# Adding up queries and keys by quarters in a two-level Winograd projection

## The chip, the cores and the metric

The kernel runs on one core of a Trainium2 chip. A core has five engines that run beside each other, each with a queue of its own that it works off strictly in order: TensorE (PE in the profile; PEld is its loading of weights), VectorE (DVE), ScalarE (ACT), GpSimd (POOL) and SyncE (SP), which here only issues DMAs. Engines wait for one another by semaphores. The metric is the device time of one execution in microseconds, as the median of several runs.

## The reference

The reference is a transformer layer over 32 sequences of 64 tokens, 512 wide: self-attention with 32 heads of 128, cross-attention over a context of 128, and a mixture of expert biases. Only the self-attention's front part matters here:

```
q = rmsnorm((hidden @ Wq + bq).reshape(b, n, H, HD), gq)
k = rmsnorm((hidden @ Wk + bk).reshape(b, n, H, HD), gk)
v = (hidden @ Wv + bv).reshape(b, n, H, HD)
attn = softmax(einsum("bnhd,bmhd->bhnm", q, k) * HD ** -0.5)
out = einsum("bhnm,bmhd->bnhd", attn, v) @ Wo + bo
```

`rmsnorm` divides by the root of the mean of the squares over the 128 numbers of a head. All of it is float32.

## The kernel before, in words

The 2048 tokens are split into two halves of 1024, a half into two units of 512 tokens (`t` = 0 and 1). The 32 heads are taken in 16 groups of two (`hg`). For each half and each group the kernel makes queries, keys and values of both units. Group 0 of each half goes through a simpler path (`single`); the other 15 of each half, 30 in all, go through `double`, and one such pass is called a window here.

**The products.** In a window the queries and keys come from a matrix product in two levels of Winograd's form of Strassen's scheme: seven products instead of eight outside, and again seven inside each. `Window.project` runs the outer products in four rounds, n = 0 to 3: products 1 and 5, then 2 and 6, then 7 and 3, then 4 alone. `Window.outer` runs the inner ones of each round in four steps, m = 0 to 3. A place (n, m) in this text is step m of round n. In each step TensorE multiplies into one or two of three PSUM banks (`p_w` in the profile, line 655), and VectorE takes a bank over into the unit's tile `qk` in SBUF: `keep` (line 666) adds the bank to what another part of the tile already holds, `end` (line 679) adds a bank to the place itself. Inside a round the bank `pa` is not cleared between products: TensorE adds the next product to what is in it. So it may not go on with `pa` before `keep` has read it. In round 3 this is so between place (3, 0), whose `keep` reads `pa`, and place (3, 1), whose first product is added to it.

A unit's `qk` tile has four places of 128 x 512: place 2h + ab holds head h, half ab of the unit's tokens; the first 256 of the 512 numbers are queries (j = 0), the last 256 keys (j = 1). A quarter of the result of a round is one t and one j.

**The outer sums.** Winograd's scheme ends with sums over whole results: place 2 takes place 3 in, and then place 3 takes place 1 in. `add` does this after round 2: for unit 0 on GpSimd, for unit 1 on VectorE (both line 734, 128 x 512). Then `squares` (ScalarE, line 356) squares each place, and at the window's end TensorE adds the squares up over a head (`ms_w`, line 779), from which the roots for `rmsnorm` come. Round 3 changes place 1 only, in place: the `keep` of (3, 0) for t = 0, j = 0 writes what GpSimd's second sum reads.

**What sets the order.** The orders on PE, VectorE, ScalarE and GpSimd are written out by hand: each engine gets its instructions in the order in which the Python code calls them. After each step of `outer`, `project` first calls what the dictionary `behind` holds for the place, then one piece of waiting work (`take_waiting`: scaling of queries for an earlier unit on VectorE, line 544, or a part of a softmax), and then what `plan` holds for it: `v`, one of the seven steps of the values' product (`values`, lines 387, 403 and 407), `line.scale` (keys of an earlier unit times their roots on GpSimd, line 542), `line.turn`, or `make`, which has GpSimd work out sums of the next group's weights (lines 120 and 152 to 155). In a window's round 2, `line.scale` is called at (2, 0), and `make` at (2, 3), where four sums of 128 x 384 are left over (lines 152 to 155). In group 1, sums of the input (lines 345 and 346 on GpSimd) are called at (2, 1) too. In group 15 there are no weight sums at (2, 3).

The values use a PSUM bank `va` in the same way: ScalarE's copy (`keep` in `values`, line 403) must have read it before TensorE goes on in it. The values' third step, at (2, 2), has such a copy, and the fifth, at (3, 0), goes on in the bank; the fifth has one again, and the sixth, at (3, 1), goes on in it.

Of the kernel before, what the change touches and what calls it, by code (L numbers as in the profile page):

```python
# [10 lines left out]
ALU = mybir.AluOpType  # L11
# [30 lines left out]
def decoder_layer(  # L42
# [228 lines left out]
    def take_waiting():  # L271
        if waiting:
            waiting.pop(0)()
# [80 lines left out]
    def square(of, name, part=1):  # L354
        sq = squares_tile(f"sq{name}", part)
        nc.scalar.activation(sq, of, AF.Square)  # L356
        return sq
# [266 lines left out]
    class Window:  # L624
# [86 lines left out]
        def project(self, plan):  # L711

            units, hg = self.units, self.w.hg
            for unit in units:
                unit.qk_tiles()
            sq = self.sq = {}

            def of(places):
                return lambda t, j: units[t].all[:, places, j, :]

            def twice(place):
                return lambda t, j: (
                    units[t].all[:, place, j, :].unsqueeze(1).to_broadcast([P, 2, QT])
                )

            def squares(h, ab, t):
                sq[h, ab, t] = square(
                    units[t].qk[h, ab], f"{h}{ab}_{units[t].name}", ab
                )

            def add(t, to, what):
                qk = units[t].qk
                on = nc.vector if t else nc.gpsimd
                on.tensor_tensor(qk[to], qk[to], qk[what], ALU.add)  # L734


            behind = {
                (1, 3): lambda: [squares(0, 0, t) for t in range(2)],
                (2, 2): lambda: (
                    add(0, (1, 0), (1, 1)),  # L740
                    add(0, (1, 1), (0, 1)),
                    squares(1, 0, 0),
                ),
                (2, 3): lambda: (
                    add(1, (1, 0), (1, 1)),
                    squares(1, 1, 0),
                    squares(1, 0, 1),
                ),
                (3, 0): lambda: add(1, (1, 1), (0, 1)),
                (3, 1): lambda: squares(1, 1, 1),  # L750
                (3, 2): lambda: squares(0, 1, 0),
                (3, 3): lambda: squares(0, 1, 1),
            }
            for n, args in enumerate(
                (
                    ((1, 5), of(slice(2, 4)), None, lambda j: bqd[:, j, bass.ts(hg, HG)]),
                    ((2, 6), of(slice(0, 3, 2)), twice(2)),
                    ((7, 3), of(slice(1, 3)), twice(2)),
                    ((4,), of(slice(1, 2)), of(slice(1, 2))),
                )  # L760
            ):

                banks = [self.bank(f"p{n}{i}") for i in range(3)]
                turned = [banks[(2 * n + i) % 3] for i in range(3)]
                for m, _ in enumerate(self.outer(args[0], turned, *args[1:])):
                    behind.get((n, m), lambda: None)()
                    take_waiting()
                    for it in plan[n][m]:
                        it()
# [489 lines left out]
    for n, (hg, half) in enumerate(groups):  # L1259
        w = weights.pop(n)  # L1260
        units = [HeadGroup(hg, 2 * half + t, w) for t in range(2)]
# [230 lines left out]
```

## Time and profile before

| | us |
|---|---|
| three runs: median (lowest to highest) | 1933.31 (1930.85 to 1934.56) |
| the profiled execution: its time | 1932.7 |
| the profiled execution: span from first to last instruction | 1930.9 |
| PE busy | 1887.6 (98%) |
| DVE busy | 1228.4 (64%) |
| POOL busy | 1044.3 (54%) |
| ACT busy | 646.8 (33%) |

A row of a group of instructions reads: line, engine, operation, what is written from what, count | busy time in all, mean of one in ns | idle time just before them, and what ended it. A row of the timeline reads: start in us from the span's start, time taken, engine, line, operation, count, and in brackets the idle time before it and what ended that. A row of the waits reads: who, for whom, us in total, times, longest. The start of an instruction in the timeline is when its engine took it up. Two instructions of one engine that follow each other overlap a little there, by some 0.05 to 0.1 us.

### The profile page before, as it was taken

How to read it: one execution, taken by the hardware profiler on the slowest of the kernel's cores; microseconds unless marked ns; L12 is line 12 of the kernel's file. 1: busy time of each engine (PE TensorE's matmuls, PEld its weight loads, DVE VectorE, ACT ScalarE, POOL GpSimd, SP SyncE). 2: the span in 40 equal slices, each digit the busy share in tenths (PEclk: the TensorE clock that was granted, in tenths of full speed). 3: DMA queues.
4: the chain of work that ended last, by engine and by line, in shares of the span. 5: the costliest groups of instructions: out<-in, count | busy, mean ns of one | idle time of the engine just before them, and what ended most of it. 6: DMA issues, size and time to landing. Idle time of an engine off the chain costs nothing.

```text
span 1930.9 us, 40526 instructions
## 1 busy us (share of the span) xinstructions
PE 1887.6 (98%) x16877; PEld 1622.2 (84%) x16877; DVE 1228.4 (64%) x2024; ACT 646.8 (33%) x1579; POOL 1044.3 (54%) x812
## 2 busy tenths in 40 slices
PE   9999999999999999999999999999998999999997
PEld 8888888888888888888888888888886888888874
DVE  7867777676667659666666666666454545554554
ACT  2343344344333443344333434433311202221122
POOL 5856666665667539665666666565234323332320
PEclk9999999999999999999999999999998999999998
DMA  4244334334433343334433333444932231223100
GB/s 138 67 134 142 121 126 129 110 105 131 133 111 110 107 140 107 99 101 131 133 110 111 110 100 100 130 134 137 301 127 86 90 111 67 71 88 112 49 20 23
DMA packets 164568, 214.92 MB, mean 111 GB/s; under 512 B 10144, under 2 KB 135136, under 8 KB 160288
## 3 DMA queue, kind: packets, MB, share of 16 engines
q1 hardware_dynamic: 163200, 211.24, 34.1%
q8 instruction: 133, 2.18, 0.5%
q10 hardware_dynamic: 1184, 1.08, 0.2%
q14 instruction: 51, 0.42, 0.1%
HBM read 171.92 MB, written 40.37 MB: 110 GB/s over the span
## 4 chain that ended last, share of the span: by engine, by line
PE 76%; DVE 12%; POOL 7%; issue 3%; DMA 1%; ACT 1%; SPq 0%; POOLq 0%; DVEq 0%; ACTq 0%
PE p_w L655 24%; PE py L837 19%; PE va L387 7%; PE vb L387 6%; POOL qk L734 5%; PE ms_w L779 3%; PE s L555 3%; PE o L592 3%; DVE qk L666 3%; DVE qk L679 3%; DVE qk L544 1%; PE pt_p L249 1%; PE pa L445 1%; DVE sums L262 1%; PE py_x L1050 1%
## 5 line engine op out<-in xcount | busy, mean ns | idle before, releaser
L655 PE MATMUL p_w<-x,w 128*128 128x256 f32 x2940 | 723.9, 383 | 8.6 <-DVE qk L666 8.0
L655 PEld LDWEIGHTS p_w<-x,w 128*128 128x128 f32 x2940 | 521.2, 190 | 70.7 <-DVE qk L666 13.1
L666 DVE TENSOR_TENSOR qk<-p_w,qk 128x512 f32<-128x512 f32 x360 | 213.0, 600 | 135.0 <-PE p_w L655 99.1
L356 ACT ACTIVATE sq<-qk 128x512 f32<-128x512 f32 x256 | 158.1, 629 | 400.2 <-POOL qk L734 225.4
L387 PEld LDWEIGHTS va<-w,x 128*128 128x128 f32 x2048 | 263.6, 191 | 30.5 <-ACT v L403 20.6
L387 PE MATMUL va<-w,x 128*128 128x128 f32 x2048 | 276.1, 278 | 2.1 <-ACT v L403 2.1
L837 PE MATMUL py<-wo,a 128*128 128x256 f32 x1152 | 262.5, 381 | 0.0
L679 DVE TENSOR_TENSOR qk<-p_w,qk 128x512 f32<-128x512 f32 x360 | 220.1, 620 | 57.4 <-PE p_w L655 53.9
L120 POOL TENSOR_TENSOR w<-w 128x768 f32<-128x768 f32 x126 | 244.5, 1951 | 2.4
L837 PEld LDWEIGHTS py<-wo,a 128*128 128x128 f32 x1152 | 213.9, 190 | 35.6 <-issue 7.3
L265 POOL TENSOR_TENSOR prob<-prob,inv 128x512 f32<-128x512 f32 x64 | 75.3, 1177 | 294.9 <-DVE inv L264 291.7
L542 POOL TENSOR_TENSOR qk<-qk,rs 128x512 f32<-128x512 f32 x128 | 172.4, 1347 | 113.1 <-DMA rs<-row_w 92.9
L387 PEld LDWEIGHTS vb<-w,x 128*128 128x128 f32 x1536 | 201.4, 192 | 9.7
L387 PE MATMUL vb<-w,x 128*128 128x128 f32 x1536 | 202.4, 275 | 0.0
L403 ACT COPY v<-va 128x256 f32<-128x256 f32 x256 | 94.8, 370 | 308.9 <-PE va L387 308.7
L544 DVE SCALAR_TENSOR_TENSOR qk<-qk,gqk,rs 128x512 f32<-128x512 f32 x128 | 173.4, 1355 | 11.1 <-DMA rs<-row_w 10.0
L837 PE MATMUL py<-wo_t,a 128*128 128x256 f32 x608 | 144.3, 389 | 0.0
L837 PEld LDWEIGHTS py<-wo_t,a 128*128 128x128 f32 x608 | 116.1, 195 | 16.9 <-issue 0.8
L734 POOL TENSOR_TENSOR qk<-qk 128x512 f32<-128x512 f32 x60 | 90.7, 1511 | 61.1 <-DVE qk L679 58.7
L257 DVE TENSOR_REDUCE mx<-s 128x8 f32<-128x512 f32 x64 | 44.1, 689 | 106.8 <-PE s L555 106.8
L407 DVE TENSOR_TENSOR v<-vb,v 128x256 f32<-128x256 f32 x192 | 80.8, 421 | 45.6 <-PE vb L387 27.0
L607 ACT ACTIVATE ot<-o,bvt 128x256 f32<-128x256 f32 x256 | 99.2, 469 | 2.2 <-PE o L592 2.2
(182 smaller groups left out, 2198.2 us busy)
## 6 DMA issues: line engine op xcount, KB each, us to landing
rs<-row_w SPq DMA_DIRECT2D x120, 512.0 KB
mixed<-ot SPq DMA_DIRECT2D x64, 512.0 KB
a<-mixed SPq DMA_DIRECT2D x32, 1024.0 KB
w<-in_wq_dram SPq DMA_DIRECT2D x64, 256.0 KB
w<-in_wk_dram SPq DMA_DIRECT2D x62, 256.0 KB
w<-in_wv_dram SPq DMA_DIRECT2D x62, 256.0 KB
wo<-in_wo_dram SPq DMA_DIRECT2D x8, 1024.0 KB
x<-in_x_dram SPq DMA_DIRECT2D x20, 256.0 KB
```

Of the source, the lines that this page charges most:

```text
L120: on.tensor_tensor(*(it.rearrange("p c j d -> p (c j) d") for it in (out, a, b)), ALU.subtract)
L356: nc.scalar.activation(sq, of, AF.Square)
L387: nc.tensor.matmul(to[:, j, :], left[i][:, c, j, :], right[i][:, c, 2, :], start=first and j == 0 and c == 0, stop=c == 1, skip_group_chec ...
L403: nc.scalar.copy(self.v[h, ab], what)
L542: nc.gpsimd.tensor_tensor(k, k, rk, ALU.mult)
L544: lambda: nc.vector.scalar_tensor_tensor(q, q, gqk, rq, ALU.mult, ALU.mult)
L607: nc.scalar.activation(ot[:, h, :, b * SEQ : (b + 1) * SEQ], o[b][:, h, :, :], AF.Identity, bias=bvt[:, hg * HG + h : hg * HG + h + 1],)
L655: nc.tensor.matmul(bank[:, s, :], self.w.inner[o][i], inner_x[self.half, o][i], start=first and s == 0, stop=True, skip_group_check=True,)
L666: nc.vector.tensor_tensor(to(t, j), bank, add(t, j), ALU.add)
L679: nc.vector.tensor_tensor(to(t, j), bank, to(t, j), ALU.add)
L734: on.tensor_tensor(qk[to], qk[to], qk[what], ALU.add)
L837: nc.tensor.matmul(py, a[:, g, :], b[g // KH][:, g % KH, :], start=n == 0 and g == 0, stop=n == last and g == NHG - 1,)
```

## The change

`add` gets an argument j and takes one half of a place, 128 x 256, instead of the whole. The sums of unit 0 (GpSimd) are called for j = 0 after (2, 1) and for j = 1 after (2, 2). Those of unit 1 (VectorE) are called one after (2, 2), two after (2, 3) and one after (3, 0). The squares of places 2 and 3 of unit 0 move from (2, 2) and (2, 3) to (2, 3) together; that of place 2 of unit 1 moves from (2, 3) to (3, 0).

```diff
-            def add(t, to, what):
-                qk = units[t].qk
+            def add(t, j, to, what):
+
+                to, what = (units[t].qk[it][:, j, :] for it in (to, what))
                 on = nc.vector if t else nc.gpsimd
-                on.tensor_tensor(qk[to], qk[to], qk[what], ALU.add)
+                on.tensor_tensor(to, to, what, ALU.add)
 
 
             behind = {
                 (1, 3): lambda: [squares(0, 0, t) for t in range(2)],
+                (2, 1): lambda: (
+                    add(0, 0, (1, 0), (1, 1)),
+                    add(0, 0, (1, 1), (0, 1)),
+                ),
                 (2, 2): lambda: (
-                    add(0, (1, 0), (1, 1)),
-                    add(0, (1, 1), (0, 1)),
-                    squares(1, 0, 0),
+                    add(0, 1, (1, 0), (1, 1)),
+                    add(0, 1, (1, 1), (0, 1)),
+                    add(1, 1, (1, 0), (1, 1)),
                 ),
                 (2, 3): lambda: (
-                    add(1, (1, 0), (1, 1)),
+                    add(1, 1, (1, 1), (0, 1)),
+                    add(1, 0, (1, 0), (1, 1)),
+                    squares(1, 0, 0),
                     squares(1, 1, 0),
+                ),
+                (3, 0): lambda: (
+                    add(1, 0, (1, 1), (0, 1)),
                     squares(1, 0, 1),
                 ),
-                (3, 0): lambda: add(1, (1, 1), (0, 1)),
                 (3, 1): lambda: squares(1, 1, 1),
                 (3, 2): lambda: squares(0, 1, 0),
                 (3, 3): lambda: squares(0, 1, 1),
```

## The prediction

> **What bounds the kernel now.** I read the shares of the page first, then the waits, then the timeline of one window.
>
> ```profile
> PE 1887.6 (98%) x16877; PEld 1622.2 (84%) x16877; DVE 1228.4 (64%) x2024; ACT 646.8 (33%) x1579; POOL 1044.3 (54%) x812
> ```
>
> TensorE bounds the kernel; any change outside it can only win what TensorE waits. The waits name the place (who, for whom, us, times, longest):
>
> ```profile
> DVE qk L666 <- POOL qk L734: 34.8, 30, 1.2
> PEld va L387 <- ACT v L403: 20.6, 60, 1.5
> PEld p_w L655 <- DVE qk L666: 13.1, 32, 1.0
> PE p_w L655 <- DVE qk L666: 8.0, 31, 0.9
> ```
>
> There are 30 windows, so each `keep` of place (3, 0) waits 1.16 us for GpSimd's outer sum, and TensorE waits in turn. The timeline of one of them (rows left out):
>
> ```profile
> 1324.77 3.12 POOL L734 TENSOR_TENSOR qk<-qk 128x512 f32<-128x512 f32 x2 [2.15 <-DVE qk L679]
> ...
> 1325.34 0.69 DVE L666 TENSOR_TENSOR qk<-p_w,qk 128x512 f32<-128x512 f32 x1 [0.65 <-PE p_w L655]
> ...
> 1326.03 1.03 PE L655 MATMUL p_w<-x,w 128*128 128x256 f32 x4
> 1326.07 0.69 DVE L734 TENSOR_TENSOR qk<-qk 128x512 f32<-128x512 f32 x1
> 1326.07 0.63 ACT L356 ACTIVATE sq<-qk 128x512 f32<-128x512 f32 x1 [6.47 <-POOL qk L734]
> 1326.61 0.35 ACT L403 COPY v<-va 128x256 f32<-128x256 f32 x1
> ...
> 1327.01 1.16 PE L387 MATMUL va<-w,x 128*128 128x128 f32 x8
> 1327.84 1.00 POOL L152 TENSOR_TENSOR w<-w 128x384 f32<-128x384 f32 x1
> ...
> 1327.92 0.42 DVE L666 TENSOR_TENSOR qk<-p_w,qk 128x256 f32<-128x256 f32 x1 [1.16 <-POOL qk L734]
> ...
> 1328.40 1.13 PE L655 MATMUL p_w<-x,w 128*128 128x256 f32 x4 [0.22 <-DVE qk L666]
> ...
> 1329.38 1.16 PE L387 MATMUL va<-w,x 128*128 128x128 f32 x8
> ...
> 1330.37 1.03 PE L655 MATMUL p_w<-x,w 128*128 128x256 f32 x4
> ```
>
> The PE rows are places (3, 0), its `v`, (3, 1), its `v`, and (3, 2). Undisturbed, four `p_w` products are followed 0.87 us later by the next group, and eight `va` ones 0.89 us later (as 1325.14 to 1326.03, a `v` step on the bank `vb`). So (3, 2) could start at 1326.03 + 2 x (0.87 + 0.89) = 1329.55; it starts at 1330.37. **0.82 us a window are lost here**: 0.11 since the copy at 1326.61 stands behind a square that waits for GpSimd, 0.50 for the `keep`, 0.11 for starting again after it, 0.10 at the second `v`, whose copy (1328.97) is behind two more squares. 28 of the 30 windows show these offsets within 0.05 us; the two of group 1 have offsets of their own. No gain can exceed some 30 x 0.82 = 25 us.
>
> **The change, part by part.** The orders on PE and SP stay; no DMA moves.
>
> *Squares one place on.* At (2, 2) the copy no longer has a square ahead of it, so the 0.11 go. At (3, 0) its successor now stands behind the square of unit 1's place 2, which waits for VectorE's sum; that copy must end by the second `v`.
>
> *Halves on GpSimd.* A 128x256 sum takes 0.73 us there (its input sum at 78.42 us), a 512 one 1.27; the split costs 2 x (2 x 0.73 - 1.27) = 0.4 us a window, on an engine that is idle for 2.15 us ahead of the old sums. The first two halves fit in: in the old timeline VectorE's scaling ends at 1323.16, so they run behind it until 1323.16 + 0.59 + 0.08 + 0.73 = 1324.56. The `keep` of (3, 0) needs only these. Its 1.16 us wait for GpSimd's data is gone.
>
> *Halves on VectorE.* These are the price. Two of the halves now stand directly ahead of that `keep` in VectorE's queue, while GpSimd, done sooner, goes on to its weight sums. What that does is shown where two 128x256 sums of VectorE follow each other beside the same weight sums:
>
> ```profile
> 738.66 1.73 POOL L542 TENSOR_TENSOR qk<-qk,rs 128x512 f32<-128x512 f32 x1
> 739.19 1.49 DVE L342 TENSOR_TENSOR x<-x 128x256 f32<-128x256 f32 x1
> 740.36 1.18 POOL L152 TENSOR_TENSOR w<-w 128x384 f32<-128x384 f32 x1
> 740.60 1.23 DVE L343 TENSOR_TENSOR x<-x 128x256 f32<-128x256 f32 x1
> 741.62 1.06 POOL L153 TENSOR_TENSOR w<-w 128x384 f32<-128x384 f32 x1
> ```
>
> L342 takes 1.49 us instead of 0.41 (L342 at 725.18, alone): it ends 0.29 us after L542 does (740.68 against 740.39). L152 ends 0.86 us after L342, L343 0.28 us after L152. Each holds off the other for a whole instruction, and they take turns in the order in which they asked. [...] Without that rule the sums would lie side by side, nothing would be late, and the change would be worth the whole 0.82 us a window; with it I lay the window out again, with the waits of the row above:
>
> - `end` pair over at 1324.69. First VectorE half from 1324.62, alone, 0.41: 1325.03.
> - GpSimd's third half asks at 1324.77, gets in at 1325.03, + 0.59 (L345 after L342 at 77.0 us): 1325.62. Its fourth, + 0.08 + 0.73: 1326.43.
> - VectorE's `keep` of (2, 3) as before, to 1326.03. Its second half asks at 1325.95, waits for the fourth half, + 0.28: 1326.71.
> - L152 asked at 1326.39, gets in: + 0.86, 1327.57. VectorE's third half asked at 1326.63: waits, + 0.28, 1327.85.
> - `keep` of (3, 0) from 1327.78, + 0.42: 1328.20. TensorE goes on 0.06 later, as before: 1328.26 instead of 1328.40.
> - The square of unit 1 from 1327.95 (0.1 after its sum, as at 1329.56 before), 0.63; the copy behind it ends at 1328.85. The second `v` starts at 1328.26 + 0.98 = 1329.24 with its weights loaded in time, so (3, 2) follows after 0.89: 1330.13 instead of 1330.37.
>
> So 0.24 us in each of the 26 plain windows: 6.2 us. What is late next is the fourth VectorE half: it asks at some 1328.66, waits for L153 until 1327.85 + 0.86 = 1328.71, ends at 1328.99, sooner than the whole one did (1328.79 + 0.68). The `keep`s of (3, 1), which (3, 2) needs, follow the values' addition and come at 1329.3 to 1330.05, the first 0.4 us ahead of its need.
>
> *Group 15* (two windows) has no weight sums there, so the third half runs at once, and the `keep` ends by 1327.4, before TensorE asks (1327.79): 2 x 0.82 = 1.6 us.
>
> *Group 1* (two windows) has GpSimd's two input sums between its first and second quarter, 2 x 0.73 us ahead of the squares' inputs. Three squares then stand before the copy that the second `v` needs. Laid out in the same way the window of 774.41 us loses 0.5; bounds are a gain of 0.8 and a loss of 1.5. I take 2 x 0.5 = 1.0 lost.
>
> Sum: 6.2 + 1.6 - 1.0 = 6.8 us. The profiled execution took 1932.7 (span 1930.9), which would be 1925.9; its distance from the median is 0.6 us, within the runs' 3.7. From the median: 1933.3 - 6.8 = **1926.5 us**.
>
> **The rivals.**
>
> *No turns taken: the full gain.* If VectorE kept GpSimd out between its second and third half, the `keep` would end by 1327.4 and the change would win 0.82 in 28 windows and nothing in group 1: 23 us, 1910. For it: the halves follow each other with no wait between. Against it: at 739 us, and at 75 us beside the input sums, GpSimd got in between just such a pair.
>
> *Nothing to be seen.* The 0.14 us at the `keep` is a difference of six hops; if each is 0.03 longer, and the group 1 windows lose 1.5 each, 26 x 0.06 + 1.6 - 3 leaves nothing: 1933. That the `keep` should still wait for all of GpSimd's halves would not matter: they are over by 1326.43.
>
> *Slower: GpSimd gets two turns.* If L152 asks before VectorE's second half does, that half waits for L152 too, and the third for L153: the `keep` ends at some 1329.1 and (3, 2) starts 0.7 us later than now. 26 x 0.7 - 1.6 + 1.0 = 18 us more: 1951. It decides once GpSimd's fourth half ends before some 1325.99, when L152 would ask ahead of 1325.95; I have 1326.43, so 0.44 us in hand. For it: at 1225.35 us, VectorE's scaling asked 0.03 us after a weight sum and waited 1.79 us for it. Against it: nothing can start the third half before the `end` pair is over.
>
> **How the numbers follow.** The likeliest, 60%: 0.24 a window give or take 0.1, group 1 give or take 1 us: 1923 to 1930.5. The full gain 12%, 1907 to 1913. Nothing to be seen 14%, 1929.5 to 1937. Slower, 14%, 1937 to 1955. A range from 1908 to 1936 leaves out the slower case and the edges of two others, some 18%. Less than 0.2% (3.9 us) can't be told from no change. Faster than 1929.4 is nine tenths of the likeliest and the full gain: 66%; within 0.2%, the rest of the likeliest and the third: 20%; slower 14%.
>
> **What would show it.** The wait of the `keep` for GpSimd's sum (34.8 us) is gone. VectorE's sums come as 120 of 128x256: in a plain window one of 0.4 us, then two of 0.8 and 1.2 with L152 between them. The `keep` still makes TensorE wait at (3, 1), some 0.1 us less than the 0.22; the copy at (2, 2) makes it wait no more. In group 15's windows no such wait is left. I am wrong if a second weight sum stands between VectorE's two halves, if the period of windows (42.34 us) falls by 0.8, or if TensorE waits longer for the copy at (3, 1).

## The result, and the profile after

The changed kernel takes 1925.84 us (median of 5, 1923.92 to 1927.75) where the kernel before took 1933.31. The quotient of these two medians is 0.9961; the comparison of the runs gives a ratio of 0.9967, with a 95% interval from 0.9956 to 0.9978, and in a later session, on one chip with the kernel before, 0.9961 (0.9947 to 0.9976). It is 0.3 to 0.4% faster; 1926.5 had been forecast.

The page of the profile after shows the first line's shares again:

```profile
PE 1875.2 (98%) x16877; PEld 1627.6 (85%) x16877; DVE 1257.8 (65%) x2084; ACT 653.1 (34%) x1579; POOL 1054.9 (55%) x872
```

VectorE and GpSimd have 60 instructions more each and are busy for 29 and 11 us longer, and the kernel is faster. The waits of the kernel after (who, for whom, us, times, longest) show where TensorE still stands:

```profile
PEld p_w L655 <- DVE qk L666: 15.2, 29, 1.6
PE p_w L655 <- DVE qk L666: 10.8, 31, 1.4
PEld va L387 <- ACT v L403: 4.2, 2, 2.5
```

The `keep` of (3, 0) no longer waits for GpSimd's sum: its row of 34.8 us is gone. The wait for the copy at line 403 fell from 60 times to 2, both in group 1. But TensorE's wait for the `keep` did not shrink, it grew from 8.0 to 10.8 us. Of this, 1.44 us are one wait in the last window, which is no part of the change (see "The change again"); in each plain window the wait grew from 0.22 to 0.28 us. The timeline of a plain window says why (place (3, 0) begins at 1320.14; line 735 is `add` now; rows left out):

```profile
1318.72 0.41 DVE L735 TENSOR_TENSOR qk<-qk 128x256 f32<-128x256 f32 x1
1318.88 1.65 POOL L735 TENSOR_TENSOR qk<-qk 128x256 f32<-128x256 f32 x2 [0.21 <-DVE qk L679]
...
1320.06 1.89 DVE L735 TENSOR_TENSOR qk<-qk 128x256 f32<-128x256 f32 x2
1320.14 1.03 PE L655 MATMUL p_w<-x,w 128*128 128x256 f32 x4
1320.48 1.19 POOL L152 TENSOR_TENSOR w<-w 128x384 f32<-128x384 f32 x1
...
1321.00 1.05 PE L387 MATMUL va<-w,x 128*128 128x128 f32 x8
1321.75 1.06 POOL L153 TENSOR_TENSOR w<-w 128x384 f32<-128x384 f32 x1
1321.87 0.41 DVE L666 TENSOR_TENSOR qk<-p_w,qk 128x256 f32<-128x256 f32 x1
...
1322.34 1.13 PE L655 MATMUL p_w<-x,w 128*128 128x256 f32 x4 [0.28 <-DVE qk L666]
...
1323.30 1.05 PE L387 MATMUL va<-w,x 128*128 128x128 f32 x8
...
1324.19 1.03 PE L655 MATMUL p_w<-x,w 128*128 128x256 f32 x4
```

VectorE's second and third half, 0.41 us each when alone, take 1.89 us together. The second takes 0.75 us: it waits for GpSimd's fourth half and ends at 1320.80, 0.28 us after it. Then GpSimd's L152 gets its turn, and the third takes 1.22 us and ends at 1321.95, 0.28 us after L152. So the `keep` starts only at 1321.87. Seen from the start of (3, 0), the places lie as follows (us, plain windows):

| | before | forecast | after | nothing late |
|---|---|---|---|---|
| the values' step | 0.99 | 0.87 | 0.87 | 0.87 |
| (3, 1) | 2.37 | 2.23 | 2.20 | 1.76 |
| its values' step | 3.35 | 3.21 | 3.17 | 2.63 |
| (3, 2) | 4.34 | 4.10 | 4.06 | 3.52 |

The values' step now starts 0.12 us sooner and takes 1.05 us instead of 1.16 in the timeline, so it ends 0.23 us sooner; (3, 1) starts only 0.17 us sooner. TensorE comes to the wait earlier and so waits 0.06 us longer, though it is let go earlier. A wait's length alone does not tell whether a stage got shorter.

By stretches of the two profiled executions (a window is counted to the start of its sums of squares):

| us | before | after | difference |
|---|---|---|---|
| start, group 0 and group 1 of the first half | 95.72 | 97.35 | +1.63 |
| group 2 of the first half | 41.41 | 41.34 | -0.07 |
| groups 3 to 14 of the first half, 12 windows | 508.09 | 504.64 | -3.45 |
| group 15 | 42.34 | 41.51 | -0.83 |
| groups 0 and 1 of the second half | 95.01 | 95.39 | +0.38 |
| groups 2 to 14, 13 windows | 550.53 | 546.69 | -3.84 |
| group 15 | 42.34 | 43.21 | +0.87 |
| after the windows | 555.47 | 552.20 | -3.27 |
| span | 1930.90 | 1922.33 | -8.57 |

### The profile page after: what moved, and what is told of

Read it like the earlier page. It is cut to its first block, busy times and chain, and to the rows that moved or that the text cites. A ratio compares the mean times of both kernels' runs of the same rounds, so it can differ in the third digit from the quotient of the medians.

```text
span 1922.3 us, 40625 instructions
## 1 busy us (share of the span) xinstructions
PE 1875.2 (98%) x16877; PEld 1627.6 (85%) x16877; DVE 1257.8 (65%) x2084; ACT 653.1 (34%) x1579; POOL 1054.9 (55%) x872
## 4 chain that ended last, share of the span: by engine, by line
PE 86%; DVE 8%; issue 2%; POOL 2%; DMA 1%; ACT 1%; SPq 0%; POOLq 0%; DVEq 0%; ACTq 0%
PE p_w L655 31%; PE py L846 19%; PE va L387 10%; PE vb L387 7%; PE ms_w L788 3%; PE s L555 3%; PE o L592 3%; DVE qk L666 2%; PE pt_p L249 1%; PE pa L445 1%; DVE qk L735 1%; PE e_x L1022 1%; PE py_x L1059 1%; PE pt_x L249 1%; PE pl_f L1078 1%
## 5 line engine op out<-in xcount | busy, mean ns | idle before, releaser
L655 PE MATMUL p_w<-x,w 128*128 128x256 f32 x2940 | 723.7, 383 | 11.3 <-DVE qk L666 10.8
L387 PEld LDWEIGHTS va<-w,x 128*128 128x128 f32 x2048 | 268.4, 192 | 17.1 <-ACT v L403 4.2
L387 PE MATMUL va<-w,x 128*128 128x128 f32 x2048 | 270.1, 275 | 3.4 <-ACT v L403 3.4
L735 POOL TENSOR_TENSOR qk<-qk 128x256 f32<-128x256 f32 x120 | 103.1, 860 | 10.4 <-DVE qk L679 5.7
```

What stands on the lines that cost most here:

```text
L387: nc.tensor.matmul(to[:, j, :], left[i][:, c, j, :], right[i][:, c, 2, :], start=first and j == 0 and c == 0, stop=c == 1, skip_group_chec ...
L655: nc.tensor.matmul(bank[:, s, :], self.w.inner[o][i], inner_x[self.half, o][i], start=first and s == 0, stop=True, skip_group_check=True,)
L735: on.tensor_tensor(to, to, what, ALU.add)
```

## The experiments

All were timed against the kernel before in interleaved runs. "Period" is from one window's sums of squares to the next, in plain windows. The ratio is that of the comparison of the runs, and need not be the quotient of the two medians.

| kernel | median us | ratio to before (95%) | period, us | (3, 2) after (3, 0), us |
|---|---|---|---|---|
| before | 1931.95 to 1934.29 | 1 | 42.34 | 4.34 |
| the change again | 1924.85 | 0.9961 (0.9947 to 0.9976) | 42.06 | 4.06 |
| e1 halves only | 1926.88 | 0.9967 (0.9956 to 0.9978) | 42.05 | 4.06 |
| e2 squares only | 1932.65 | 0.9998 (0.9987 to 1.0010) | 42.34 | 4.34 |
| e3 wide sum between | 1925.17 | 0.9963 (0.9950 to 0.9976) | 42.32 | 4.32 |
| e4 GpSimd halves | 1913.73 | 0.9903 (0.9886 to 0.9920) | 41.51 | 3.51 |
| e5 VectorE halves | 1926.51 | 0.9967 (0.9955 to 0.9980) | 42.06 | 4.07 |
| e6 third half later | 1906.32 | 0.9862 (0.9839 to 0.9885) | 41.51 | 3.51 |
| e7 e4, group 1's squares | 1908.41 | 0.9874 (0.9859 to 0.9889) | 41.51 | 3.51 |
| e8 e6, group 1's squares | 1905.30 | 0.9856 (0.9838 to 0.9874) | 41.51 | 3.51 |
| e9 e8, wide sum later | 1903.76 | 0.9849 (0.9831 to 0.9867) | 41.51 | 3.51 |

### The change again

> The changed kernel once more. Its first profile had three things away from the outer sums that the layout does not know: 1.0 us lost before the first window, a wait of 1.7 us for a row of roots in the last window, and 3.3 us won after the last window. If these are scatter of one execution, they come out differently here, while plain windows keep their period of 42.05 us and group 1's two windows stay some 0.4 to 0.6 us longer than before from place (3, 0) to the sums of squares. If they belong to the change, they come again. Time 1926 us, give or take 2.

The plain windows repeat: 42.06 us. What was lost ahead of the windows is scatter: up to (3, 0) of the first of them the kernel before took 87.68 us, the change 88.72 and 88.33, and e2, with whole sums as before, 89.15. The wait in the last window did not come again: in the first profile VectorE's scaling waited there for a row of roots, and the `keep` behind it held TensorE up (timeline of the changed kernel's first profile):

```profile
1342.75 1.86 DVE L544 SCALAR_TENSOR_TENSOR qk<-qk,gqk,rs 128x512 f32<-128x512 f32 x1 [3.46 <-DMA rs<-row_w]
...
1345.27 1.99 PE L655 MATMUL p_w<-x,w 128*128 128x256 f32 x8 [1.44 <-DVE qk L666]
```

In the second profile the last window took 41.51 us, as the other one of group 15. The wait came again in the last window of e4 (42.90), e5 (43.25) and e9 (43.12), and not in e1, e3, e6, e7 or e8: a landing that is sometimes late, not a part of the change. The 3.3 us after the windows are no part of it either: that stretch took 552.2 to 553.3 us in some profiles (after, the change again, e3, e5, e9) and 555.3 to 556.3 in others (before, e1, e2, e4, e6, e7, e8). Group 1 of the first half took 10.26 us from (3, 0) to its sums of squares, 1.6 more than in the first profile; that is told in the last section.

### e2: the squares alone

```diff
                 (2, 2): lambda: (
                     add(0, (1, 0), (1, 1)),
                     add(0, (1, 1), (0, 1)),
-                    squares(1, 0, 0),
                 ),
                 (2, 3): lambda: (
                     add(1, (1, 0), (1, 1)),
+                    squares(1, 0, 0),
                     squares(1, 1, 0),
-                    squares(1, 0, 1),
                 ),
-                (3, 0): lambda: add(1, (1, 1), (0, 1)),
+                (3, 0): lambda: (
+                    add(1, (1, 1), (0, 1)),
+                    squares(1, 0, 1),
+                ),
```

> Whole sums as before, squares called where the change calls them. Theory (the copy's delay at (2, 2) lies inside the longer wait for the keep, and at (3, 0) the copy stands behind the same squares as before): the values' step follows (3, 0) after 0.87 us instead of 0.99, but (3, 1) still starts 2.37 us after (3, 0); period 42.34 us, no difference, 1933 us. Rival (the squares' order is worth its 0.11 us): period 42.2 us, 1930 us. Other rival (the copy at (3, 0) comes later): up to 42.45 us, 1936 us.

Period 42.34, ratio 0.9998: nothing. The values' step follows (3, 0) after 0.87 us, so the copy at (2, 2) was freed, and (3, 1) starts at 2.37 as before. The 0.11 us lay inside the wait for the `keep`.

### e1: the halves alone

The change, with its squares put back to the places that `-` has in e2's diff.

> Halves on both engines as in the change, squares called where they were before. Theory (the halves carry the whole gain; once GpSimd's third half is early, the square at (2, 2) no longer delays the copy behind it): (3, 2) starts 4.05 us after (3, 0), period 42.05 us in plain windows, 1926 us give or take 2. Rival (moving the squares is what freed the copy): the start of the values' step after (3, 0) stays 0.99 us after it instead of 0.87, period 42.15 to 42.25 us, 1929 to 1931 us.

Plain windows are those of the change to 0.01 us: there the halves carry all of it. In group 1 the old places cost something: 10.60 and 10.37 us from (3, 0) to the sums of squares, where before had 8.04 and 7.90 and the change 8.63 and 8.28 (10.26 and 8.27 in its second profile); a part of it is a low clock behind the wait in both windows (the mean granted clock of this execution is 0.989, that of the change's first profile 0.994), as in the last section. The two medians, 1926.88 and 1924.85, are of different sessions, and their ratios' intervals overlap.

### e5 and e4: the halves of one engine

e5 gives VectorE halves and GpSimd its two whole sums after (2, 2); e4 the other way round (`None` takes the whole place):

```diff
 # e4, against the change
                 (2, 2): lambda: (
                     add(0, 1, (1, 0), (1, 1)),
                     add(0, 1, (1, 1), (0, 1)),
-                    add(1, 1, (1, 0), (1, 1)),
                 ),
                 (2, 3): lambda: (
-                    add(1, 1, (1, 1), (0, 1)),
-                    add(1, 0, (1, 0), (1, 1)),
+                    add(1, None, (1, 0), (1, 1)),
...
                 (3, 0): lambda: (
-                    add(1, 0, (1, 1), (0, 1)),
+                    add(1, None, (1, 1), (0, 1)),
```

> Halves on VectorE alone; GpSimd makes its two whole sums after (2, 2) as before; squares as in the change. Theory (turns in order of asking): VectorE's second half follows GpSimd's first whole sum, its third follows GpSimd's second, which ends 1.53 us after (3, 0) begins; that is where line 152's sum ended in the change. So the keep comes at the same time: period 42.05 to 42.1 us, 1926 us: beside VectorE's halves, GpSimd's win nothing. Rival (the gain of the change comes from GpSimd's halves): period 42.34 us or more, 1933 us or more.

> Halves on GpSimd alone; VectorE keeps its two whole sums at (2, 3) and (3, 0); squares as in the change. Theory (VectorE's halves cost what is missing to the full gain, since GpSimd's weight sum gets a turn between the second and the third of them): with one whole sum there is no second turn before the keep of (3, 0). It asks while GpSimd's fourth half runs, ends some 0.85 us after place (3, 0) began, the keep is done before TensorE needs it, and (3, 2) starts 3.52 us after (3, 0): period 41.5 us in plain windows, time some 1911 us. Rival (the keep is late for another reason, and the halving of VectorE's sums is harmless or helps): period 42.05 us or more, 1926 us or more.

Both came as the theory had it. With VectorE's halves the period is 42.06 whether GpSimd's sums are halved or not; with GpSimd's halves alone it is 41.51, which is all that these places had to give. Only in group 15, where no weight sum comes in between, do GpSimd's halves count beside VectorE's: (3, 2) follows (3, 0) after 4.06 and 4.07 us there in e5, and after 3.51 in the change. The timeline of e4, where (3, 0) begins at 1309.40:

```profile
1308.14 1.54 POOL L736 TENSOR_TENSOR qk<-qk 128x256 f32<-128x256 f32 x2 [0.21 <-DVE qk L679]
...
1309.43 0.79 DVE L736 TENSOR_TENSOR qk<-qk 128x512 f32<-128x512 f32 x1
1309.64 1.46 POOL L152 TENSOR_TENSOR w<-w 128x384 f32<-128x384 f32 x1
...
1310.15 0.41 DVE L666 TENSOR_TENSOR qk<-p_w,qk 128x256 f32<-128x256 f32 x1
...
1311.16 1.03 PE L655 MATMUL p_w<-x,w 128*128 128x256 f32 x4
```

(Line 736 is `add` in this kernel.) The whole sum asks at 1309.43, takes 0.79 us instead of 0.69 behind GpSimd's fourth half, and is over at 1310.22. L152 asked at 1309.64 and stands behind it (it ends at 1311.10, 0.88 us after the sum), but nothing that the `keep` needs stands behind L152 any more. The `keep` starts 0.75 us after (3, 0), not 1.73, and (3, 1) starts without a wait. One long operation was 1 us better here than two short ones.

### e6: the third half behind the `keep`

```diff
                 (2, 3): lambda: (
                     add(1, 1, (1, 1), (0, 1)),
-                    add(1, 0, (1, 0), (1, 1)),
                     squares(1, 0, 0),
                     squares(1, 1, 0),
                 ),
-                (3, 0): lambda: (
-                    add(1, 0, (1, 1), (0, 1)),
-                    squares(1, 0, 1),
-                ),
-                (3, 1): lambda: squares(1, 1, 1),
-                (3, 2): lambda: squares(0, 1, 0),
+                (3, 0): lambda: add(1, 0, (1, 0), (1, 1)),
+                (3, 1): lambda: (
+                    add(1, 0, (1, 1), (0, 1)),
+                    squares(1, 0, 1),
+                ),
+                (3, 2): lambda: (
+                    squares(1, 1, 1),
+                    squares(0, 1, 0),
+                ),
```

> The change, with VectorE's third half called at (3, 0), behind the keep, its fourth at (3, 1), and unit 1's squares one place on again. Theory (the third half ahead of the keep is the whole of the loss that is left): the keep has only the second half before it, is done before TensorE asks, and (3, 2) starts 3.52 us after (3, 0); period 41.5 us, 1911 us give or take 3. Rival (the second half, or the fourth in front of the keeps of (3, 1), holds it up as well): period 41.7 to 42.0 us, 1916 to 1925 us.

Period 41.51: four halves on VectorE are harmless as soon as the third isn't ahead of the `keep`. The time is 5 us below what was expected, outside its 3 us. The profiled execution is the slowest of the four, 1910.6 us, so its stretches don't say what the others did better; this stays open. (Its stretch after the windows took 555.3 us, the longer of the two times that occur; whether the others had the shorter one isn't shown.) Its timeline (where (3, 0) begins at 1305.82):

```profile
1305.73 0.75 DVE L735 TENSOR_TENSOR qk<-qk 128x256 f32<-128x256 f32 x1
1306.16 1.19 POOL L152 TENSOR_TENSOR w<-w 128x384 f32<-128x384 f32 x1
1306.52 0.42 DVE L666 TENSOR_TENSOR qk<-p_w,qk 128x256 f32<-128x256 f32 x1
...
1307.39 0.42 DVE L735 TENSOR_TENSOR qk<-qk 128x256 f32<-128x256 f32 x1
1307.42 1.25 POOL L153 TENSOR_TENSOR w<-w 128x384 f32<-128x384 f32 x1
1307.57 1.03 PE L655 MATMUL p_w<-x,w 128*128 128x256 f32 x4
```

L152 runs while VectorE takes over PSUM banks, and neither shows a wait for the other: the `keep` takes 0.42 us here, and in the first profile of the change the 55 of this size that lay wholly inside an instruction of GpSimd took 0.41 to 0.42. The third half finds L152 done.

### e3: a longer sum of GpSimd in between

```diff
             for b, of in (
-                (self.w.rearrange("p k c j h d -> p c j k h d"), slice(0, 4)),
                 (self.t.rearrange("p i c j d -> p c j i d"), slice(4, 7)),
+                (self.w.rearrange("p k c j h d -> p c j k h d"), slice(0, 4)),
             ):
```

> The change, with the two blocks of weight sums in the other order: the sums at (2, 3) are 128x512 instead of 128x384, those at (1, 3) 384 instead of 512; nothing else moves. Theory (the third half of VectorE waits for the whole of line 152's sum): the sum is 0.27 us longer, so the keep of (3, 0) is 0.27 us later, (3, 1) starts 2.47 us after (3, 0) instead of 2.20, the period of plain windows is 42.3 us, and the gain over before is nearly gone: some 1932 to 1933 us. Rival (the keep waits for something else): period 42.05 us, 1926 us.

In the windows it is as the theory has it, to a hundredth. The timeline of e3, where (3, 0) begins at 1320.97:

```profile
1320.88 2.17 DVE L735 TENSOR_TENSOR qk<-qk 128x256 f32<-128x256 f32 x2
...
1321.32 1.45 POOL L152 TENSOR_TENSOR w<-w 128x512 f32<-128x512 f32 x1
...
1322.98 0.41 DVE L666 TENSOR_TENSOR qk<-p_w,qk 128x256 f32<-128x256 f32 x1
...
1323.44 1.13 PE L655 MATMUL p_w<-x,w 128*128 128x256 f32 x4 [0.55 <-DVE qk L666]
```

The two halves take 2.17 us instead of 1.89, (3, 1) starts 2.46 us after (3, 0) instead of 2.20, and the period is 42.32. **The time, though, missed its expectation**: 1925.2 us instead of 1932 to 1933. The 6.7 us that windows 3 to 14 and 2 to 14 lost against the second profile of the change (3.21 + 3.50) came back in three others: up to group 1 of the first half 94.94 us instead of 98.59, group 2 behind it 39.69 instead of 41.03, groups 0 and 1 of the second half 93.79 instead of 95.38, 6.6 us together. The sums at (1, 3) are shorter in e3, and in group 1 the squares wait for GpSimd. Its second quarter began 1.83 us after (3, 0) in the first window of group 1 in the change (first profile), and 0.45 us before it in e3 (at 88.03 against 88.48). From (3, 0) to the sums of squares the two windows took 6.47 and 7.11 us, which is 5.0 of the 6.6 us. I had thought of the plain windows alone. (1.6 us of the first of these differences is the low clock, 0.55 from 95.00 to 98.40 us, that the second profile of the change had there.)

### e7, e8 and e9: group 1

In the change's first window of group 1, three squares wait for GpSimd's second quarter and stand before the copy that TensorE needs (timeline of the changed kernel):

```profile
90.55 1.59 POOL L735 TENSOR_TENSOR qk<-qk 128x256 f32<-128x256 f32 x2
...
91.30 0.63 ACT L356 ACTIVATE sq<-qk 128x512 f32<-128x512 f32 x1 [3.77 <-POOL qk L735]
...
92.17 1.15 ACT L356 ACTIVATE sq<-qk 128x512 f32<-128x512 f32 x2 [0.24 <-POOL qk L735]
...
93.22 0.35 ACT L403 COPY v<-va 128x256 f32<-128x256 f32 x1
...
93.63 1.16 PE L387 MATMUL va<-w,x 128*128 128x128 f32 x8 [2.05 <-ACT v L403]
```

e7 is e4, and e8 is e6, with these squares moved in group 1 alone; e9 is e8 with e3's order of the weight sums. e7's edit (e8's is alike):

```diff
+            if hg == 1:
+                late = (
+                    lambda: squares(1, 0, 0),
+                    lambda: squares(1, 1, 0),
+                    lambda: squares(1, 0, 1),
+                )
+                behind[2, 3] = lambda: add(1, None, (1, 0), (1, 1))
+                behind[3, 0] = lambda: add(1, None, (1, 1), (0, 1))
+                behind[3, 1] = lambda: ([it() for it in late], squares(1, 1, 1))
```

> As e4, and in group 1 alone the three squares of (2, 3) and (3, 0) move to (3, 1), behind the copy of (3, 0). Theory (group 1 loses since three squares that wait for GpSimd's late second quarter stand before that copy): the stretch from (3, 0) to the sums of squares shortens by 1 to 2 us in each of the two windows, and the time is 2 to 4 us below that of e4. Rival (group 1 loses by GpSimd's input sums as such): no difference to e4 above 0.5 us a window.

> As e6 (VectorE's third and fourth half later), and in group 1 alone the three squares go to (3, 1), behind the copy of (3, 0), as in e7. Theory (what e6 lacks to e7 in group 1 is the wait for that copy, 2.0 and 1.5 us in e6): the two windows of group 1 come to some 6.5 and 6.8 us from (3, 0) to the sums of squares, as in e7, instead of 8.1 and 7.6; plain windows 41.51 us as in e6; time 1 to 3 us below e6's 1906.3, some 1904 us. Rival: group 1 is held by GpSimd's sums themselves where VectorE has halves, and stays at 7.6 to 8.1 us; 1906 us.

> As e8, with the two blocks of weight sums in the other order (128x512 at (2, 3), as in e3). Theory from e3 (a longer sum of line 152 costs only where a VectorE sum that the keep of (3, 0) is queued behind waits for it; the shorter sums at (1, 3) free GpSimd sooner in groups 1 and 2): plain windows stay at 41.5 us, where in e3 they went from 42.05 to 42.32; group 1 and what lies before and after it win 1 to 3 us in all over e8. Rival (the longer sums cost 0.27 us in any order of the halves): period 41.8 us, some 7 us more than e8.

From (3, 0) to the sums of squares, group 1's two windows take (us):

| before | the change | e4 | e6 | e7 | e8 | e9 |
|---|---|---|---|---|---|---|
| 8.04, 7.90 | 8.63, 8.28 | 10.45, 8.63 | 8.14, 7.64 | 6.47, 6.75 | 6.74, 6.29 | 6.23, 6.24 |

The squares before the copy were the loss: with them behind it 1.3 to 4.0 us a window are won (the 4.0 with a low clock in e4's first window, 0.52 from 95.50 to 98.90 us, as in the last section). e7 ended 5.3 us below e4, more than the 2 to 4 expected. e8 and e9 show that VectorE's halves do not hold group 1, and that the longer sums cost nothing once no half of VectorE's waits for them ahead of the `keep`. What e9 was to win over e8 in group 1 and around it was 1 to 3 us; in the profiles, up to group 2 of the first half and in groups 0 and 1 of the second, it is 0.6 us. e9 is the fastest at 1903.76 us, 1.5% below before; e8 and e6 lie within its interval, so the last steps are not told apart by the time, only by the windows.

## Why the prediction was right or wrong

- *The stage and its loss* (0.82 us a window): right. e4, e6 and their successors end at 41.51, 0.83 below 42.34, and (3, 2) comes at 3.51 where 3.52 had been worked out. The bound of 25 us drawn from it was too low, since it counted group 1 like the rest: e8 moves nothing but outer sums and squares, and ends 29.0 us below the kernel before of its session. Its windows of group 1 won 1.3 and 1.6 us; a part of the rest is not explained.
- *The squares one place on*: right as placed. The 0.11 us at the copy go, and e2 shows that they are worth nothing alone.
- *Halves on GpSimd*: right. The first quarter's fit in ahead, and the wait for GpSimd's data is gone. e5 shows that beside VectorE's halves they do nothing in plain windows, and 0.55 us in each of group 15.
- *Halves on VectorE, turns in the order of asking*: right, and shown by e3 (a sum longer by 0.27 us moves the period by 0.27), e4 and e6 (41.51 us once no third half stands ahead of the `keep`). The rival of the full gain was what happens when the turn is avoided; the rival of two turns did not occur.
- *Size of a plain window*: 0.29 us instead of 0.24. The steps of the layout came 0.03 us shorter up to (3, 1) and 0.01 from there to its values' step. 26 x 0.29 = 7.5 us instead of 6.2.
- *Group 15*: 0.83 us instead of 0.82; in the last window it was hidden in the first profile by a late row of roots, and seen in the second.
- *Group 1*: 0.59 + 0.38 = 0.97 us lost from (3, 0) on, where 1.0 was taken. It held by luck in part: the second execution lost 2.2 us in the first of them.
- *The sum*: -7.5 - 1.7 + 1.0 = -8.2 us by the measured terms, against -6.8 forecast and -7.5 between the medians (-7.1 in the second session). That the two profiled executions are 8.6 us apart, close to this sum, is partly luck: 1.0 us lost ahead of the windows and 1.7 by the late row of roots nearly cancel the 3.3 won after the windows.
- *What would show it*: one sign was wrong. TensorE's wait at (3, 1) was to fall by 0.1 us from 0.22, and rose to 0.28. The step that failed is the last of the layout: it had (3, 1) at nearly the right time (2.23 us after (3, 0), measured 2.20), but did not set it against the values' step, which ends 0.23 us sooner.

## What to carry to other kernels

Before an operation is split that takes turns with those of another engine, as VectorE's and GpSimd's sums did here, ask what gets in between the parts. Two halves in front of a deadline may each wait for an instruction of the other engine (here they took 0.75 and 1.22 us instead of 0.41); put one there, or none, and the rest behind. And read a change by when the next stage starts, not by the length of the wait before it.

## What the runs showed of the hardware

I had not expected a low clock behind waits of 2 us. In the second execution of the change, group 1's first window took 1.6 us longer with the same wait. The windows view (us, then busy time of PE, PEld, DVE, ACT and POOL, granted clock, DMA) has the stretch behind that wait, first of that execution:

```profile
95.00:98.40 3.40, 3.40 (x16) 3.07 (x15) 1.18 (x3) 0.71 (x2) 0.79 (x1) 0.55 0.00 0
```

and of the first one:

```profile
94.00:97.40 3.40, 3.40 (x30) 2.97 (x32) 1.97 (x6) 1.44 (x4) 2.12 (x3) 1.00 0.00 0
```

The granted clock is 0.55 in the one and 1.00 in the other. In the profiles of all kernels here, between 60 us and the last window, this occurs four times (the change again, e1 twice, e4). Each time the clock changes lie on a grid of 3.41 us, the low clock lasts one step of it, and in the step just before, by the starts and ends of its products in the trace, TensorE had been idle for 59, 72, 65 and 67% of the time. (In the change again the clock is 0.66 from 94 to 96 us, 0.50 from 96 to 98 and 0.99 from 98 to 100, which makes 3.40 us at 0.50. From end to end of the change's first profile, the clock's records last 3.41, 6.83 or 54.61 us or longer multiples of 3.41, but for the last one.) The most idle step that was not followed by a low clock is that of the first profile of the change, 91.79 to 95.20 us, 54%. The wait was the same 2.05 us in both; where it fell on the grid differed: 1.84 us of it lay in one step in the first profile, some 2.0 us in the second. Here a step that was 59% idle was followed by a low clock, and one of 54% was not. How far the share alone decides is not shown by four cases.
